# Two-layer cross-attention in float32: layer 0's projections and output sums moved from column halves to row halves of TensorE

## The chip, the cores and the metric

The kernel runs on one core of a Trainium2 chip. The metric is the device time of one execution in microseconds, as the median of several runs. TensorE multiplies matrices, VectorE and ScalarE do the softmax, GpSimd scales rows, and the queue of SyncE (SP) issues nearly all DMA transfers.

## The reference

Four batches of 1024 tokens with 512 features attend to a context of 1024 tokens with 384 features. Two layers follow each other, and all of it is float32:

```python
# layer 0: 16 heads of 64
h = _layernorm(x, gamma, beta)
Q, K, V = h @ Wq, context @ Wk, context @ Wv          # 1024 inner features
attn = softmax(einsum('bihd,bjhd->bhij', Q, K)) * 64 ** -0.5
x = x + einsum('bhij,bjhd->bihd', attn, V) @ Wo + bo
# layer 1: 16 heads of 32, rotated and normalised q and k
xn = x * rsqrt(mean(x * x) + 1e-5) * norm_w
q, k, v = rotate(xn @ wq), rotate(ctx @ wk), ctx @ wv
q, k = q / |q|, k / |k|
x = x + (softmax(q k^T * sqrt(32)) v) @ wout
```

## The kernel before

The work of a batch in layer 0 runs over eight pairs of heads (`p`), and for each pair over eight tiles of 128 queries (`i`): 64 steps a batch. `Attention0.step` (L376) does one step. It first issues the scores of both heads (L367). A head has 64 features, so each of the two score matmuls contracts over 64 rows only, and the two heads run beside each other in the two row halves of the TensorE array. The trace writes this shape 64\*128: 64 rows, 128 columns. The scores take both score tiles, which is all that there is of them (`ps_s`, two buffers of two banks); the next step's scores wait until this step's two exponentials have read them.

Then VectorE takes the negative maximum of each row (L392), ScalarE the exponential and its sum (L393), VectorE the reciprocal (L397), and GpSimd scales the row (L398). In the next step VectorE transposes the result in squares of 32 (L401). After every second step `regroup` (L407) issues 16 DMA copies (L412) that complete the transposition of a block of two query tiles into `eT`. In an odd step, once two blocks wait, `product` (L420) multiplies the older one by the values (L428). That matmul contracts over all 128 rows and fills 64 columns for each head: the column halves, 128\*64 in the trace.

What is left of a step is filled with other work. `Units` (L56) is a queue of small pieces, each with a cost in microseconds. `step` ends with `self.u.fill(us)` (L405): pieces are issued until the budget is used up. The main loop works out the budget as all work still to be done in layer 0, divided by the steps that are left, less the product's 3.5 us in an odd step (L804 to L807), so the fill is spread evenly over the 64 steps. The pieces are:

- keys and queries of a later pair (`pair_units`, L310; `pkT` and `pqT` in the trace), one matmul of 512 columns a piece, three pieces for each half of the keys and four for each half of the queries;
- its values (`pv`), one tile of 128 tokens a piece;
- output sums (`add_units`, L286; `po`): for each of eight token tiles two pieces, and then an addition to the row `x` on VectorE (L295). In pairs 0 and 1 they are those left over from layer 1 of the batch before, and each finished row is stored; from pair 2 on they belong to layer 0, two pairs at a time;
- in pairs 6 and 7 the first rotated keys and values of layer 1 (`rotated_chains`, L452; `value_chains`, L536).

All of these go through the helper `matmul` (L160), which cuts the output features into two column halves in layer 0 (four quarters in layer 1):

```python
        w = P // which["cols"]
        for j in range(which["cols"]):
            rr = slice(j * w, (j + 1) * w)
            nc.tensor.matmul(o[rr], lhsT[:, rr], rhs, start=start, stop=stop)
```

The results of the pieces and of `product` go to four PSUM banks that `bank` (L127) hands out in rotation. `evac` (L136) copies them out on ScalarE.

On SP's queue, in program order, stand the copies of `eT`, the weights of a pair (`pair_load`, L302, three DMAs, two buffers), the rows `x` that are loaded again in pairs 1 and 2 (`load_x`, L279), the output weights (`wo_load`) and the stores of finished rows (`store_all`, after each pair). The weights of pair `p + 1` are asked for where the work on pair `p` begins.

Of the kernel before, what the change touches and what calls it, by code (L numbers as in the profile page):

```python
# [36 lines left out]
P = 128  # L38
S = 1024
# [55 lines left out]

def weave(chains, lag):

    res = []
    for i in range(len(chains) + lag):
        if i < len(chains):  # L100
            res += chains[i][0]
        if 0 < i <= len(chains):
            res += chains[i - 1][1]
        if i >= lag:
            res += chains[i - lag][2]
    return res
# [3 lines left out]
def xattn_kernel(ctx: ExitStack, tc: tile.TileContext, a: dict, out: bass.AP):  # L110
# [14 lines left out]
    which = {"n": 0, "from": 0, "cols": 2, "kept": None}  # L125

    def bank(name):  # L127

        while True:
            which["n"] = which["n"] + 1 if which["n"] < 3 else which["from"]  # L130
            if which["n"] != which["kept"]:
                break
            which["kept"] = None
        return ps_f.tile([P, 512], F32, tag=f"f{which['n']}", name=name)
# [37 lines left out]
    def context_units(b, ct):  # L172

        raws = {}

        def load(h):
            for t in range(4 * h, 4 * h + 4):
                if b == 0 and h:
                    raws[t] = sb.tile([P, S], F32, tag="vals", bufs=4, name=f"c_{b}_{t}")[:, :DC]
                else:  # L180
                    raws[t] = sb.tile([P, DC], F32, tag="row", bufs=4, name=f"c_{b}_{t}")
                nc.sync.dma_start(raws[t], c[b, t * P : (t + 1) * P, :])

        def turn_over(h, k):
            if k == 0:
                if h == 0:
                    both = sb.tile([P, NC_, S], F32, tag="ctxT", bufs=1, name=f"cT_{b}")
                    ct.extend([both[:, :, :512], both[:, :, 512:]])
            pp = bank(f"ptc_{b}_{h}_{k}")
            for t in range(4):  # L190
                nc.tensor.transpose(pp[:, t * P : (t + 1) * P], raws[4 * h + t][:, k * P : (k + 1) * P], ident)
            evac(ct[h][:, k, :], pp)

        return [
            {
                "load": [(0.0, lambda h=h: load(h))],
                "turn": [(0.45, lambda h=h, k=k: turn_over(h, k)) for k in range(NC_)],
            }
            for h in range(2)
        ]  # L200

    def norm_units(b, layer, hT, rows):
# [39 lines left out]
        def turn_over(h, k):  # L242
            if k == 0:
                hT.append(sb.tile([P, NQ, 512], F32, tag="hT", bufs=2, name=f"hT{layer}_{b}_{h}"))
            pp = bank(f"pth{layer}_{b}_{h}_{k}")
            for t in range(4):
                nc.tensor.transpose(pp[:, t * P : (t + 1) * P], got[h][t][:, k * P : (k + 1) * P], ident)  # L247
            if layer == 0:
                nc.scalar.activation(  # L249
                    hT[h][:, k, :], pp, AF.Identity, bias=cols[:, 1, k : k + 1], scale=cols[:, 0, k : k + 1]  # L250
                )
            else:
                nc.scalar.activation(hT[h][:, k, :], pp, AF.Copy, scale=cols[:, 2, k : k + 1])

# [31 lines left out]
    def add_units(xt, lhs, w, name, cs, then=None):  # L286

        n = len(cs)

        def one(t, i, pp=[None]):  # L290
            if i == 0:
                pp[0] = bank(f"{name}_{t}")
            matmul(pp[0], lhs(cs[i])[:, t * P : (t + 1) * P], w(cs[i]), i == 0, i == n - 1)
            if i == n - 1:
                nc.vector.tensor_add(xt[t], xt[t], pp[0])  # L295
                if then is not None:
                    then(t)

        return [[(0.86, lambda t=t, i=i: one(t, i)) for i in range(n)] for t in range(NT)]

# [9 lines left out]
    def pair_units(b, p, w, hT, ct, res):  # L310
# [3 lines left out]
        def project(what, src, w0, nk, h, k, st={}):  # L314
            if what == "kT" and h == 0 and k == 0:
                qk = sb.tile([P, 2, S], F32, tag="qk", bufs=3, name=f"qk0_{n}")
                res["kT"], res["qT"] = qk[:, 0], qk[:, 1]
            if k == 0:
                st["pp"] = bank(f"p{what}0_{n}_{h}")
            matmul(st["pp"], w()[:, w0 + k, :], src[h][:, k, :], k == 0, k == nk - 1)  # L320
            if k < nk - 1:
                return
            if what == "qT":
                evac(res[what][:, h * 512 : (h + 1) * 512], st["pp"])
            else:
                quarters = res[what].rearrange("p (g c i) -> p c g i", g=4, i=32)
                evac(quarters[:, 4 * h : 4 * h + 4], st["pp"].rearrange("p (c g i) -> p c g i", g=4, i=32))

        def values(h, t, st={}):
            if h == 0 and t == 0:  # L330
                res["v"] = sb.tile([P, NT, P], F32, tag="v", bufs=3, name=f"v0_{n}")
            if t == 0:
                st["pp"] = bank(f"pv0_{n}_{h}")
            for k in range(NC_):
                matmul(
                    st["pp"][:, t * P : (t + 1) * P],
                    ct[h][:, k, t * P : (t + 1) * P],
                    w()[:, NQ + NC_ + k, :],
                    k == 0,
                    k == NC_ - 1,  # L340
                )
            if t == 3:
                evac(res["v"][:, 4 * h : 4 * h + 4, :].rearrange("p t f -> p (t f)"), st["pp"])
# [4 lines left out]
            "v": [(0.66, lambda h=h, t=t: values(h, t)) for h in range(2) for t in range(4)],  # L348
# [5 lines left out]
    class Attention0:  # L354


        def __init__(self, b, units):
            self.b, self.u = b, units
            self.blocks = deque()
            self.turn = self.raw = None  # L360
# [15 lines left out]
        def step(self, p, i, pr, us):  # L376
# [28 lines left out]
            self.u.fill(us)  # L405
# [14 lines left out]
        def product(self):  # L420
# [14 lines left out]
            evac(pr["vals"][:, q * W : (q + 1) * W], av[:, :W])  # L435

# [15 lines left out]
    def rotated_chains(dst, src, nk, w, name, tmp):  # L452
# [10 lines left out]
        def project(t0, i, k):  # L463
            if i == 0 and k == 0:
                tiles[t0] = [bank(f"{name}_p{t0}")]
                if which["from"] == 0:
                    which["kept"] = which["n"]
# [7 lines left out]
        def rotate(t0, pp):  # L475
# [16 lines left out]
            tiles[t0] = t1  # L492

        def turn_over(t0):
# [9 lines left out]
            nc.scalar.copy(dst()[:, :, t0 * P : (t0 + TH) * P], pt.rearrange("p (g t) -> p g t", g=2))  # L504

# [30 lines left out]
    def value_chains(v, wv, ct, name):  # L536
        def one(t0, i, k, st={}):
# [5 lines left out]
            if i == TH - 1 and k == NC_ - 1:  # L543
                pv = st["pp"].rearrange("p (t g d) -> p g t d", t=TH, g=2)
                for g in range(2):
                    nc.scalar.copy(v[g][:, t0 : t0 + TH, :], pv[:, g])

# [113 lines left out]
    def prepare_units(b):  # L661

        st = {"ct": [], "hT": [], "pairs": [{} for _ in range(NPAIR)]}
# [5 lines left out]
        def project(p):  # L669
            def begin():  # L670
                if p + 1 < NPAIR:
                    w[p + 1] = pair_load(b, p + 1)

            begin = {"begin": [(0.0, begin)]}
            return begin | pair_units(b, p, lambda: w[p], st["hT"], st["ct"], st["pairs"][p])

        st["project"] = lambda p: flat(project(p).values())
# [50 lines left out]
    for b in range(B):  # L728
        ct, hT, pairs = st["ct"], st["hT"], st["pairs"]
        xt = []  # L730
        att = Attention0(b, work)
# [4 lines left out]
        for p in range(NPAIR):  # L736
# [7 lines left out]
            other = []  # L744
            if p < 2:
                other = tail[p * len(tail) // 2 : (p + 1) * len(tail) // 2]
            elif p % 2 == 0:
                i = p // 2 - 1
                outs = add_units(
# [6 lines left out]
                other = flat(outs[:4])  # L756
            else:
                other = flat(outs[4:])
            if p == 6:
                kq = {}  # L760
# [6 lines left out]
            if p == NPAIR - 1:  # L767
# [14 lines left out]
                other = k[2][0] + k[1][2] + flat(last)  # L782
                values = [(0.0, begin_v)] + vs[0][0] + k[3][0] + reload + k[2][2] + flat(c[0] for c in vs[1:]) + k[3][2]
            ahead = st["project"](p + 2) if p + 2 < NPAIR else []
            n = 7 * (p == 0)
            work.add(ahead[:n] + other)
            if p % 2 or other and p == 0:
                made[p + 1] = work.end()
            work.add(ahead[n:])
            if p + 2 < NPAIR:  # L790
                made[p + 2] = work.end()
            if p == 5:
                wq = []
                work.add([(0.0, lambda wq=wq: wq.append(half_q_load(0)))])
            left = sum(c for c, _ in values) if p == NPAIR - 1 else 0.0
            for i in range(NT):
                if b == 0 and p == 0 and i == 3:
                    work.until(begun)
                if left and i == 4:
                    work.add(values)  # L800
                    left = 0.0
                if 1 <= p <= 2 and i % 2 == 0:
# [3 lines left out]
                todo = work.total() + left + later + AV * ((NT * NPAIR + 1 - max(NT * p + i, 4)) // 2)  # L806
# [4 lines left out]
            if p + 1 < NPAIR:  # L811
                work.until(made[p + 1])
            else:
                work.drain()
            store_all()
# [8 lines left out]
        q = rotated_chains(lambda kq=kq: kq["q"], xnT, NQ, lambda k, wq=wq: wq[0][:, k, :], f"q1_{b}_0", tmp)  # L824
# [7 lines left out]
        which["from"], which["cols"] = 1, 4  # L832
# [63 lines left out]
        which["from"], which["cols"] = 0, 2  # L896
        if b == B - 1:
            tail = flat(adds[1][6:])
        else:
            outs = add_units(  # L900
                xt, lambda n, o=o: o[n], lambda n, w=wo1[1]: w[:, n % 2, :], f"po1_{b}_1", (2, 3), store
            )
            tail = flat(outs)
# [38 lines left out]
```

## Time and profile before

| | us |
|---|---|
| median of 3 runs | 2907.1 (2905.81 to 2908.67) |
| the profiled execution | 2903.31 |
| its span, first to last instruction | 2901.5 |
| TensorE (PE) busy | 2849.7 |
| VectorE (DVE) busy | 2189.1 |
| ScalarE (ACT) busy | 1439.5 |
| GpSimd (POOL) busy | 938.9 |

In the profile PE stands for TensorE's matmuls and PEld for its weight loads. A line of the timeline gives the start and length of a run of like instructions, the engine, the line of the kernel, the operation, what it writes and reads, its shape, and in brackets how long the engine had been idle and what ended that. The ends of matmuls are modelled; their starts are recorded, so the text works with the time from one start to the next. A matmul or weight load in float32 stands in the trace as two instructions.

### The profile page before, as it was taken

How to read it: one execution, taken by the hardware profiler on the slowest of the kernel's cores; microseconds unless marked ns; L12 is line 12 of the kernel's file. 1: busy time of each engine (PE TensorE's matmuls, PEld its weight loads, DVE VectorE, ACT ScalarE, POOL GpSimd, SP SyncE). 2: the span in 40 equal slices, each digit the busy share in tenths (PEclk: the TensorE clock that was granted, in tenths of full speed). 3: DMA queues.
4: the chain of work that ended last, by engine and by line, in shares of the span. 5: the costliest groups of instructions: out<-in, count | busy, mean ns of one | idle time of the engine just before them, and what ended most of it. 6: DMA issues, size and time to landing. Idle time of an engine off the chain costs nothing.

```text
span 2901.5 us, 66687 instructions
## 1 busy us (share of the span) xinstructions
PE 2849.7 (98%) x27336; PEld 1425.7 (49%) x27336; DVE 2189.1 (75%) x2952; ACT 1439.5 (50%) x2329; POOL 938.9 (32%) x776
## 2 busy tenths in 40 slices
PE   8999999999999999999999999999999999999998
PEld 4444455555444444555544445455554444445544
DVE  5677785877777778587777777858877777786877
ACT  4444444666444444466644444446664444444665
POOL 2343353420134335432024433534102343353400
PEclk9999999999999999999999999999999999999999
DMA  5887775010398777401039887730104887773000
GB/s 144 189 187 181 167 171 133 22 37 25 75 210 192 183 170 175 113 22 36 26 92 211 192 184 166 178 93 22 36 26 112 207 197 183 165 171 81 2 2 30
DMA packets 177552, 348.87 MB, mean 120 GB/s; under 512 B 37600, under 2 KB 93152, under 8 KB 177248
## 3 DMA queue, kind: packets, MB, share of 16 engines
q1 hardware_dynamic: 175920, 343.96, 50.1%
q8 instruction: 216, 3.54, 0.5%
q14 instruction: 88, 0.72, 0.1%
q10 hardware_dynamic: 1328, 0.66, 0.1%
HBM read 67.64 MB, written 8.39 MB: 26 GB/s over the span
## 4 chain that ended last, share of the span: by engine, by line
PE 89%; DVE 4%; ACT 3%; issue 2%; SPq 1%; DMA 1%; POOL 1%; DVEq 0%; ACTq 0%
PE s L367 16%; PE av L428 15%; PE po L165 11%; PE s L581 9%; PE pv L165 8%; PE pqT L165 7%; PE av L626 7%; PE pkT L165 5%; PE q_p L165 4%; PE k_p L165 2%; PE av L645 2%; ACT e L591 1%; SPq L412 1%; PE pth L247 1%; DMA eT<-e 1%
## 5 line engine op out<-in xcount | busy, mean ns | idle before, releaser
L392 DVE TENSOR_REDUCE m<-s 128x1 f32<-128x1024 f32 x512 | 602.9, 1219 | 372.1 <-PE s L367 371.5
L591 ACT ACTIVATE e<-s 128x1024 f32<-128x1024 f32 x512 | 496.7, 1022 | 252.5 <-PE s L581 239.5
L398 POOL TENSOR_SCALAR raw<-raw,li 128x1024 f32<-128x1024 f32 x256 | 287.1, 1122 | 725.0 <-DVE li L397 717.0
L367 PE MATMUL s<-qk 64*128 64x512 f32 x2048 | 515.6, 615 | 2.9 <-ACT e L393 2.2
L393 ACT ACTIVATE e<-s,m 128x1024 f32<-128x1024 f32 x256 | 283.1, 1110 | 465.8 <-DVE m L392 224.2
L393 ACT ACTIVATE raw<-s,m 128x1024 f32<-128x1024 f32 x256 | 285.4, 1115 | 455.0 <-DVE m L392 455.0
L428 PE MATMUL av<-eT,v 128*64 128x256 f32 x4096 | 470.1, 382 | 4.8 <-DMA eT<-e 3.6
L398 POOL TENSOR_SCALAR e<-e,li 128x1024 f32<-128x1024 f32 x256 | 287.0, 1122 | 473.7 <-DVE li L397 244.2
L600 DVE TENSOR_TENSOR both<-e 128x512 f32<-128x512 f32 x512 | 340.5, 699 | 87.2 <-ACT e L591 84.3
L428 PEld LDWEIGHTS av<-eT,v 128*64 128x64 f32 x4096 | 284.7, 137 | 225.1 <-issue 84.8
L367 PEld LDWEIGHTS s<-qk 64*128 64x128 f32 x2048 | 183.7, 186 | 281.6 <-issue 165.9
L581 PE MATMUL s<-q,k 32*128 32x256 f32 x4096 | 306.0, 401 | 5.8 <-ACT q L504 2.7
L401 DVE STREAM_TRANSPOSE e<-e 128x1024 f32<-128x1024 f32 x256 | 310.0, 1229 | 0.3
L401 DVE STREAM_TRANSPOSE e<-raw 128x1024 f32<-128x1024 f32 x256 | 310.0, 1228 | 0.2 <-DMA eT<-e 0.2
L581 PEld LDWEIGHTS s<-q,k 32*128 32x128 f32 x4096 | 192.1, 184 | 141.0 <-ACT e L591 72.0
L165 PE MATMUL pqT<-hT,w 128*64 128x512 f32 (+1 forms) x1216 | 240.6, 595 | 2.5 <-ACT hT L249 2.5
L165 PE MATMUL po<-wo,vals 128*64 128x512 f32 x1024 | 234.6, 596 | 0.0
L295 DVE TENSOR_TENSOR x<-x,po 128x512 f32<-128x512 f32 x200 | 131.7, 678 | 86.2 <-PE po L165 85.2
L165 PEld LDWEIGHTS pv<-w,cT 128*64 128x64 f32 (+1 forms) x3360 | 170.3, 132 | 41.6 <-issue 34.8
L165 PE MATMUL pv<-w,cT 128*64 128x128 f32 (+1 forms) x3360 | 184.3, 274 | 0.7 <-ACT hT L249 0.7
L165 PE MATMUL pkT<-cT,w 128*64 128x512 f32 (+1 forms) x912 | 182.4, 598 | 0.0
L602 DVE TENSOR_TENSOR both<-both 128x1024 f32<-128x1024 f32 x128 | 159.7, 1248 | 4.4
(82 smaller groups left out, 2776.1 us busy)
## 6 DMA issues: line engine op xcount, KB each, us to landing
eT<-e SPq DMA_DIRECT2D x2048, 128.0 KB, 2.4
xr<-in_x_dram SPq DMA_DIRECT2D x32, 256.0 KB, 4.0
wo<-in_Wo_dram SPq DMA_DIRECT2D x16, 512.0 KB, 4.5
x<-in_x_dram SPq DMA_DIRECT2D x32, 256.0 KB, 4.0
out_dram<-x SPq DMA_DIRECT2D x32, 256.0 KB, 2.6
w<-in_Wq_dram SPq DMA_DIRECT2D x31, 256.0 KB, 3.2
c<-in_ctx_dram SPq DMA_DIRECT2D x32, 192.0 KB, 4.2
wkv<-in_wkv_dram SPq DMA_DIRECT2D x16, 384.0 KB, 3.5
```

Of the source, the lines that this page charges most:

```text
L165: nc.tensor.matmul(o[rr], lhsT[:, rr], rhs, start=start, stop=stop)
L367: nc.tensor.matmul(sc[j][:, kb * 512 : (kb + 1) * 512], pr["qT"][r[j], i * P : (i + 1) * P], pr["kT"][r[j], kb * 512 : (kb + 1) * 512], st ...
L392: nc.vector.tensor_reduce(m[:, j : j + 1], sc[j], AX.X, ALU.max, negate=True)
L393: nc.scalar.activation(e[j], sc[j].rearrange("p (g s) -> p g s", g=4), AF.Exp, bias=m[:, j : j + 1], accum_out=l[:, j : j + 1])
L398: nc.gpsimd.tensor_scalar(e[j], e[j], li[:, j : j + 1], HD0**-0.5, ALU.mult, ALU.mult)
L401: self.turn = [lambda j=j: nc.vector.transpose(self.e[:, :, i % BQ * 2 + j, :], e[j]) for j in range(2)]
L428: nc.tensor.matmul(av[r[j], :W].rearrange("p (t a i) -> p t a i", t=BQ, a=4), pr["v"][:, k, r[j]], eT[:, j, :, :, k * 32 : (k + 1) * 32], ...
L581: nc.tensor.matmul(sc[j // 2][:, j % 2, c, :], kT[rr, g, k * P : (k + 1) * P], qT[rr, g, qb * WQ : (qb + 1) * WQ], start=True, stop=True,)
L591: nc.scalar.activation(e, sc[u], AF.Exp, scale=float(np.sqrt(np.float32(HD1))))
L600: nc.vector.tensor_add(into[:, 2 * u : 2 * u + 2, :], es[u][:, :, 0, :], es[u][:, :, 1, :])
L602: nc.vector.tensor_add(acc, acc, into)
L626: nc.tensor.matmul(self.av[rr, 0, :], v[g][:, 2 * kk + c, rr], es[j // 2][:, j % 2, c, :], start=first and c == 0, stop=end and c == 1,)
```

## The change

The keys and queries of pairs 2 to 7 and the output sums of pairs 0 to 5 are issued in another form and at other places.

- A *duo* makes two outputs at once, each in its own bank: both token halves of a pair's keys or queries, or two token tiles of the output sums. The contraction over 128 rows is cut into two row halves. In the duo's first half one output takes rows 0 to 63 and the other rows 64 to 127, in the array's two row halves; in the second half they change places. The number of matmuls stays the same.
- A duo's first half is issued in the gap of one even step and its second half in the gap of the next even step, before the first half of the duo that follows. The two banks stay taken over the odd step between. At the end both outputs are copied on ScalarE, or added to `x` on VectorE.
- Even steps then hold duo halves, odd steps the product and one piece of the old queue (two if over four are waiting). The duos begin at step 2 of a batch, in batch 0 at step 10; before that and after the last duo the old rule fills the steps. The value pieces of pair `p + 2` join the queue at step 3 of pair `p`.
- The values of a pair come in pieces of two token tiles, each with a bank and a copy of its own.
- `bank` hands out the bank that was released longest ago; `let_go` releases one when the instruction that empties it has been issued.
- The weights of a pair are asked for when the work of the pair before in the same buffer has been issued (`then`, run at the next fill). Layer 1's first half of `wq` is asked for after pair 6's work. Stores are issued at the start of even steps.
- In pairs 6 and 7 the pieces stand in another order, and the first values of layer 1 join the queue at step 3 of pair 7 in place of 4.

```diff
+class Duos:
+    SLOT = 0.86
...
+    def half(self, i):
+        n, f = self.open
+        f(i)
+        if i:
+            self.open = None
+        return n * self.SLOT
+
+    def fill(self):
+        us = self.half(1) if self.open else 0.0
+        if self.todo:
+            self.open = self.todo.popleft()
+            us += self.half(0)
+        return us
...
     def bank(name):
-        while True:
-            which["n"] = which["n"] + 1 if which["n"] < 3 else which["from"]
-            if which["n"] != which["kept"]:
-                break
+        if free[0] == which["kept"] and len(free) > 1:
+            free.rotate(-1)
             which["kept"] = None
+        which["n"] = free.popleft()
...
+    def let_go(pp):
+        free.append(taken.pop(id(pp))[0])
...
+    def duo(names, n, lhsT, rhs, close):
+        pps = []
+        def half(i):
+            if i == 0:
+                pps.extend(bank(name) for name in names)
+            for k in range(n):
+                for t in range(2):
+                    o = t ^ i
+                    rr = slice(t * 64, (t + 1) * 64)
+                    nc.tensor.matmul(
+                        pps[o], lhsT(o, k)[rr], rhs(o, k)[rr], start=i == 0 and k == 0, stop=i == 1 and k == n - 1
+                    )
+            if i == 1:
+                for o in range(2):
+                    close(o, pps[o])
+                    let_go(pps[o])
+        return n, half
...
-            "v": [(0.66, lambda h=h, t=t: values(h, t)) for h in range(2) for t in range(4)],
+            "v": [(1.32, lambda h=h, t=t: values(h, t)) for h in range(2) for t in (0, 2)],
+            "duos": [project_duo("kT", ct, NQ, NC_), project_duo("qT", hT, 0, NQ)],
...
-            self.u.fill(us)
+            self.fill(i % BQ, us)
...
+            def then():
+                if 1 <= p < NPAIR - 2:
+                    st["due"].append(lambda: w.update({p + 2: pair_load(b, p + 2)}))
+                elif p == NPAIR - 2:
+                    st["due"].append(lambda: st["wq"].append(half_q_load(0)))
...
+        def fill(odd, us, b=b, duos=duos, st=st):
+            while st["due"]:
+                st["due"].popleft()()
+            if not duos.begun:
+                work.fill(us)
+            elif odd:
+                for _ in range(min(1 + (len(work.todo) > 4), len(work.todo))):
+                    work.one()
+            else:
+                alone = not duos.open
+                work.owed = us - duos.fill()
+                if alone or not duos.open:
+                    work.fill(0.0)
...
-                other = k[2][0] + k[1][2] + flat(last)
-                values = [(0.0, begin_v)] + vs[0][0] + k[3][0] + reload + k[2][2] + flat(c[0] for c in vs[1:]) + k[3][2]
+                other = k[2][0] + k[1][2] + flat(last[:2]) + k[3][0] + flat(last[2:]) + k[2][2]
+                values = [(0.0, begin_v)] + vs[0][0] + reload + vs[1][0] + k[3][2] + vs[2][0] + vs[3][0]
...
+                ahead = st["project"](p + 2)
+                duos.add(ahead["duos"][:1] + sums[:1] + ahead["duos"][1:] + sums[1:])
...
+                if i == 3 and p < NPAIR - 2:
+                    work.add(ahead["v"])
+                    made[p + 2] = work.end()
+                    left = 0.0
...
+                if i % 2 == 0:
+                    store_all()
...
+                duos.begun = duos.total() > 0 and NT * p + i >= (2 if b else NT + 2)
```

## The prediction

> **What bounds the kernel now.** I read the page first: engines, granted clock, chain.
>
> ```profile
> PE 2849.7 (98%) x27336; PEld 1425.7 (49%) x27336; DVE 2189.1 (75%) x2952; ACT 1439.5 (50%) x2329; POOL 938.9 (32%) x776
> PEclk9999999999999999999999999999999999999999
> PE 89%; DVE 4%; ACT 3%; issue 2%; SPq 1%; DMA 1%; POOL 1%; DVEq 0%; ACTq 0%
> ```
>
> TensorE (PE) is the bound, at full clock. A busy PE is not a PE at its peak, so next the timeline of one even and one odd step of layer 0 (columns: start, length).
>
> ```profile
> 299.33 1.99 PE L367 MATMUL s<-qk 64*128 64x512 f32 x8
> 299.87 0.19 PEld L367 LDWEIGHTS s<-qk 64*128 64x128 f32 x2 [0.24 <-issue]
> 300.30 0.19 PEld L367 LDWEIGHTS s<-qk 64*128 64x128 f32 x2 [0.23 <-issue]
> 301.25 4.51 PE L165 MATMUL pqT<-hT,w 128*64 128x512 f32 x20
> 302.16 0.14 PEld L165 LDWEIGHTS pqT<-hT,w 128*64 128x64 f32 x2 [0.28 <-issue]
> 302.59 0.14 PEld L165 LDWEIGHTS pqT<-hT,w 128*64 128x64 f32 x2 [0.28 <-issue]
> ...
> 305.69 1.99 PE L367 MATMUL s<-qk 64*128 64x512 f32 x8
> ...
> 307.61 3.67 PE L428 MATMUL av<-eT,v 128*64 128x256 f32 x32
> ...
> 311.11 1.48 PE L165 MATMUL pv<-w,cT 128*64 128x128 f32 x24
> ...
> 312.52 1.99 PE L367 MATMUL s<-qk 64*128 64x512 f32 x8
> ```
>
> The trace has every f32 matmul twice; matmuls run in pairs, and the weight loads tick at 0.43 us a pair in both shapes, 64\*128 (row halves) and 128\*64 (column halves). Scores are 4 pairs, 1.72 us, but take 1.92 from start to start; pqT is 10 pairs, 4.30, and takes 4.44 (299.33, 301.25, 305.69). So going into row halves and back costs 0.20 + 0.14, about 0.35 us. In the odd step: 0.20, av 3.50 against 16 pairs of 0.2165 (3.46), pv 1.41 against 12 of 0.109 (1.31): again 0.34. From av to pv, both in column halves, nothing is lost. Each of the 64 steps of a batch pays one such round trip: 22 us a batch.
>
> The next view asks how short a step can be when PE has little to do:
>
> ```profile
> 1144.29 2.21 PE L367 MATMUL s<-qk 64*128 64x512 f32 x8
> ...
> 1145.47 1.26 DVE L295 TENSOR_TENSOR x<-x,po 128x512 f32<-128x512 f32 x2
> 1146.43 3.67 PE L428 MATMUL av<-eT,v 128*64 128x256 f32 x32
> 1146.65 2.35 DVE L392 TENSOR_REDUCE m<-s 128x1 f32<-128x1024 f32 x2
> ...
> 1149.05 1.10 ACT L393 ACTIVATE e<-s,m 128x1024 f32<-128x1024 f32 x1
> 1150.03 2.25 PE L367 MATMUL s<-qk 64*128 64x512 f32 x8
> ```
>
> With av alone the step takes 5.74: the score tiles come free only after the second exponential. The reduces began 2.36 after the scores instead of 2.02 (299.33 to 301.35 in the step above), held by the x sums; without that the step is 5.40. I use 5.45; the ends are 5.40 and 5.74. Last, batch 1's opening and PE's wait list:
>
> ```profile
> 755.65 4.81 PE L165 MATMUL pv<-w,cT 128*64 128x128 f32 x84
> ...
> 763.01 4.46 PE L165 MATMUL pkT<-cT,w 128*64 128x512 f32 x20
> ```
> ```profile
> PE av L428 <- DMA eT<-e: 3.6, 2, 2.5
> ```
>
> Today the opening gaps are full, because fill is spread evenly over all 64 steps.
>
> **The change, part by part.** Numbers of steps are within a batch, 0 to 63.
>
> *Switches removed.* With duos begun, an even step has scores and duo halves, all in row halves; only odd steps switch. Duos run from step 2 in batches 1 to 3 and from step 10 in batch 0, one opened per even step: 24 duos a batch (6 of keys, 6 of queries, 12 of sums), 20 in batch 0. The last is opened at step 48 and closed at 50, where column units follow. So even steps 2 to 48 lose their trip (24), and step 1 has no fill at all (25); batch 0 loses 20. That is 95 × 0.35 = 33.2 us off the path.
>
> *What a duo half costs.* Matmuls are as many as before. I take 0.43 a pair, from the scores rows. Here a rule speaks against the change: the Trainium skill, TensorE: Matmul & The Clock Gate, section Part 3: Packing small matmuls, says that a weight load overlaps matmuls in flight only when its row group differs. Each duo pair reloads both row groups, as do the scores, at 0.186 a load. By the rule each pair would cost up to 0.186 more; there are 12 pairs in a key duo, 16 in a query duo, 8 in a sum duo: 264 a batch, 232 in batch 0, 1024 in all: 190 us more. By the trace it is nothing: the scores pairs above reload the same halves and still tick at 0.43. I take 0.
>
> *Gaps that run dry.* Now I count what is left to fill. Even gaps hold two halves: 1.72 + 2.58 or 1.72 + 3.44; even steps are 6.02 or 6.88. An odd step is 1.72 + 3.46 + one value unit (12 pairs, 1.31) + 0.35 = 6.84. Both exceed 5.45. But in batches 1 to 3 step 0 takes all four waiting value units, so step 1 has scores alone (1.72), step 2 a first half alone (4.30), step 3 one value unit and no av yet (3.38): short of 5.45 by 3.73 + 1.15 + 2.07. Pair 6's step 54 has three units (4.65): 0.80. That is 7.75 a batch. In batch 0 it is steps 8 (one value unit, 2.07), 10 (a first half, 1.15) and 54 (0.80): 4.0. Total 3 × 7.75 + 4.0 = 27.3 us given back. With 5.74 it is 32, with 5.40 it is 26.5.
>
> A second rule bears on step 1, where PE rests 3.5 us. The same page, Part 1, says that an idle window of some 3.4 us halves the clock until a busy one has passed. PE's waits of 2.45 us (35.37 to 37.82) and 2.50 us (before the av at 105.44) left the clock at 0.999. By the rule, up to 1.7 us in each of three batches, 5 in all; by the trace 0. I take 0 and keep 5 for the range.
>
> *Banks.* The half that opens takes the banks of the odd step's av and value unit; their copies end long before. The av takes the first bank of the duo just closed: by keys or queries it is copied 6.33 after the even step's scores began (ACT is free at 5.75, a copy is 0.58), by sums it is added at 7.4 (DVE's own chain ends at 6.76, two adds 1.26); av starts at 6.02 + 1.92 = 7.94 or later. So 0. If that cover of 0.5 is gone, PE stands at av with the value unit and the next scores behind it, once per pair.
>
> *DVE.* Two x sums come together and hold DVE until 8.02; the next reduce can start at 8.04. A delay is covered by the odd step's 6.84 against 5.45. Cost 0.
>
> *Value units* are split: two ACT copies near 0.38 instead of one of 0.58, ACT 50% busy: 0. *SP.* Pair loads now go when the previous pair of that buffer is finished, stores at even steps, the half Wq load a pair later. The order on SP stays: 16 copies of eT (10.0 us from 6.78 after the scores, 2.4 to land, so 19.2) with weights (1.7), x (0.6) and stores (0.6) between them; av needs them three steps later plus 1.92: 20.8 to 22.5 in the steady part, 18.8 at step 5 and 18.4 at batch 0's step 11. That gives new waits of 0.4 to 1 at the first and 1 to 3 at the second. Before, such waits were 2.50 in batch 0 and 1.11 in batch 2 (the list's 3.6), and 1.1 put down to issue: 4.7. I set old against new: 0, with ±4.
>
> *Last two pairs.* The steps around the rotated keys are stretched now by waits for the turned tiles and the rotation on DVE: in batch 1, 6.33 for av alone (1117.02 to 1123.35) and 8.20 for the step after. Summed against pairs × pitch, about 2.3 a batch, 1.2 in batch 0: 8 us. The new order puts a turn 2 to 4 steps behind its projection and starts the last values at step 59. I take half of it: −4; bounds 0 and −8.
>
> **Sum.** −33.2 + 27.3 + 0 − 4 = −9.9 us. The profiled execution was 2903.3 (span 2901.5, 1.8 around it), 3.8 below the median 2907.1. Against the median: 2897.
>
> **The rivals.** *A wash (0.21).* Starved steps cost 5.74 and the tail's waits stay: −33.2 + 32 = −1: 2906, own range 2901 to 2913. For it: the starved step shown took 5.74, and the one beside a rotation 6.33. Against it: steps 1 to 3 have no x sums or rotation.
>
> *The duo halves are slower than the scores (0.24).* The one mechanism that ends slower: a duo pair accumulates into a bank that the other row half used, with fresh weights, and no row of the trace does that. Place: every even gap. Price: 1024 pairs. It decides at 10 ns a pair (of 430), which eats the gain; at 16 ns it is slower by 0.2%, at 22 ns 2910 + 9 = 2919. For it: the rule above. Against it: column pairs accumulate at 0.43 and row pairs reload at 0.43.
>
> *More than the sum (0.10).* All 8 us of the tail's waits and the 5 of eT go too: −33.2 + 27.3 − 13 = −19: 2888.
>
> *The change does not do what it says*: if column work slipped into even gaps the switches would stay. The fill rule sends column units to an even step only when no duo is open, so I give this nothing of its own.
>
> **How the numbers follow.** My forecast 0.45: 2897, own range 2889 to 2901. Measurement can tell about 0.2%, 5.8 us. Faster by more: forecast and the third rival, less 0.02 for the forecast's upper edge: 0.53. Within: the wash, 0.22. Slower: 0.25. Range for 8 in 10: 2882 to 2919, down past the third rival, up to the slower one's 22 ns.
>
> **What would show it.** Right: in even steps of pairs 1 to 5 the duo's matmuls appear as 64\*128 right after the scores, scores take 1.72 to the next start, and even steps are 6.0 and 6.9; odd ones 6.8. Scores to scores in steps 1 to 3 near 5.45. Wrong: weight loads of duos ticking above 0.43; PE waiting at av for ACT or DVE; a granted clock below full after step 1; steps 1 to 3 above 5.8.

## The result, and the profile after

| | us |
|---|---|
| kernel before, median of 12 runs | 2909.9 |
| changed kernel, median of 12 runs | 2911.3 (2905.8 to 2916.0) |
| ratio | 1.0007, 95% interval 0.9998 to 1.0016 |
| profiled execution after | 2905.83 |
| its span | 2904.0 |

No difference that can be measured, where 10 us of gain were forecast. The page after:

```profile
PE 2831.5 (98%) x27336; PEld 1505.8 (52%) x27336; DVE 2186.0 (75%) x2952; ACT 1447.7 (50%) x2393; POOL 936.5 (32%) x776
PEclk9999999999999999999999999999999999999999
PE 85%; SPq 4%; DVE 4%; ACT 2%; issue 2%; DMA 2%; POOL 1%; ACTq 0%; DVEq 0%
```

PE is busy 18 us less and the span is 2.5 us longer, so PE waits more. The chain says for whom: SP's queue (SPq) and DMA rise from 1% each to 4% and 2%. An even and an odd step of the steady part, in the timeline:

```profile
287.17 1.99 PE L485 MATMUL s<-qk 64*128 64x512 f32 x8
288.99 1.88 PE L356 MATMUL po<-wo,vals 64*128 64x512 f32 x8
288.99 0.19 PEld L356 LDWEIGHTS po<-wo,vals 64*128 64x128 f32 x2 [0.23 <-issue]
289.42 0.19 PEld L356 LDWEIGHTS po<-wo,vals 64*128 64x128 f32 x2 [0.24 <-issue]
...
290.71 3.60 PE L356 MATMUL pqT<-hT,w 64*128 64x512 f32 x16
...
294.14 1.88 PE L485 MATMUL s<-qk 64*128 64x512 f32 x8
...
295.95 3.67 PE L546 MATMUL av<-eT,v 128*64 128x256 f32 x32
...
299.46 1.48 PE L206 MATMUL pv<-w,cT 128*64 128x128 f32 x24
...
300.87 1.99 PE L485 MATMUL s<-qk 64*128 64x512 f32 x8
```

Weight loads tick at 0.43 in the duo too. The even step lasts 6.97 (287.17 to 294.14) for 16 pairs, 6.88; the odd one 6.73. In the kernel before the two were 6.36 for 14 pairs, 6.02, and 6.83: together they have lost one round trip, as was meant. What remained in the forecast were the starved steps, in which PE has too little to do, and the waits. Batch 1's step 1, scores alone:

```profile
759.73 1.99 PE L485 MATMUL s<-qk 64*128 64x512 f32 x8
...
763.06 1.11 ACT L511 ACTIVATE e<-s,m 128x1024 f32<-128x1024 f32 x1 [2.85 <-DVE m L510]
...
764.17 1.10 ACT L511 ACTIVATE e<-s,m 128x1024 f32<-128x1024 f32 x1
...
764.32 2.65 PE L485 MATMUL s<-qk 64*128 64x512 f32 x7 [2.61 <-ACT e L511]
```

It lasts 4.59: the next scores begin when the first exponential has freed one tile, and do not wait for the second. But the second tile comes later, and the step that follows pays for it, as after batch 0's step 8:

```profile
81.69 1.99 PE L485 MATMUL s<-qk 64*128 64x512 f32 x8
83.61 1.53 PE L206 MATMUL pv<-w,cT 128*64 128x128 f32 x24
86.29 3.11 PE L485 MATMUL s<-qk 64*128 64x512 f32 x8 [1.15 <-ACT raw L511]
```

Step 8 lasts 4.60, and in step 9 PE stands 1.15 us among the scores. The rows of PE's wait list for av, before (its other row, 3.6, stands in the prediction) and after, and SP's (total, times, longest):

```profile
PE av L428 <- issue: 1.1, 1, 1.1
```
```profile
PE av L546 <- DMA eT<-e: 8.8, 7, 2.7
PE av L546 <- DVE m L510: 6.8, 3, 3.0
PE av L546 <- DMA x<-in_x_dram: 0.7, 1, 0.7
PE av L546 <- DVE x L370: 0.5, 1, 0.5
PE av L546 <- issue: 0.2, 1, 0.2
```
```profile
SPq L324 <- DMA out_dram<-x: 22.3, 12, 2.7
```

Together 4.7 before and 17.0 after. The second row of after names VectorE, which had long been done; it is the same wait for eT, as the place shows: all these waits fall on step 11 of batch 0 and on steps 5, 11, 15 and 23 of batches 1 to 3. SP's line is new: 12 times a reload of `x` held the queue until the store out of the same buffer had landed. Batch 1's step 20, first SP, then PE:

```profile
877.82 11.14 SPq L530 DMA_DIRECT2D eT<-e  x16
889.07 0.52 SPq L391 DMA_DIRECT2D w<-in_Wk_dram  x1
...
890.98 0.99 SPq L990 DMA_DIRECT2D out_dram<-x  x2
894.72 0.34 SPq L324 DMA_DIRECT2D x<-in_x_dram  x1
895.16 10.04 SPq L530 DMA_DIRECT2D eT<-e  x16
```
```profile
903.70 1.88 PE L485 MATMUL s<-qk 64*128 64x512 f32 x8
908.03 3.67 PE L546 MATMUL av<-eT,v 128*64 128x256 f32 x32 [2.45 <-DVE m L510]
```

The copies of step 20 (its scores began at 883.89) could have started 6.78 later, at 890.67. They started at 895.16, behind weights, two stores and a reload that stood at the head of the queue from 891.97 to 894.72. Three steps on, the av stands 2.45 us. In the same trace three waits of PE were followed by 3.41 us at half clock: two such waits for eT (2.71 in batch 0, 3.02 in batch 3) and the 2.61 after batch 2's step 1. Three windows around step 23 of batch 3 (a plain step, the wait, what follows), and one after batch 2's step 1; the third number from the end is PE's granted clock:

```profile
2327.06:2333.79 6.73, 6.73 (x67) 4.16 (x63) 5.38 (x8) 3.19 (x7) 2.92 (x3) 1.00 0.75 236
2340.76:2345.66 4.90, 1.88 (x11) 0.61 (x7) 3.37 (x5) 0.03 (x1) 0.99 (x1) 1.00 0.89 209
2345.66:2352.26 6.60, 6.60 (x57) 5.04 (x57) 2.55 (x4) 2.65 (x5) 2.23 (x2) 0.74 0.89 217
1482.00:1488.00 6.00, 5.46 (x16) 2.39 (x18) 4.78 (x7) 2.50 (x5) 2.23 (x2) 0.72 0.00 0
```

Av and values take 6.60 here where 4.92 is usual (295.95 to 300.87). The balance, profile against profile, in us:

| | forecast | read from the two traces |
|---|---|---|
| switches | −33.2 | −33.2 |
| starved steps | +27.3 | +22 |
| waits for eT | 0 | +12.3 |
| half clock | 0 | +4.6 |
| last two pairs | −4 | −3.0 |
| sum | −9.9 | +2.7; the span grew by 2.5 |

The third column comes about as follows. *Excess* is here the time of a step beyond its pairs × pitch. Switches: 95 trips of 0.35; in steps 26 to 49 the excess fell by 4.2 a batch, over 12 even steps. Starved steps: the excess of steps 1 to 5 of batches 1 to 3 and of steps 8 to 11 of batch 0, less trips, waits for eT and half clock; about 6.2 in each of the three batches and 3.8 in batch 0. Half clock: 1.7, 1.2 and 1.7 at the three places; the half clock in the last microseconds of both executions is left out. Last two pairs: the excess of steps 50 to 62, 28.6 before and 25.6 after.

### The profile page after: what moved, and what is told of

The parts are those of the page before. It is cut to its first block, busy times and chain, and to the rows that moved or that the text cites. A ratio compares the mean times of both kernels' runs of the same rounds, so it can differ in the third digit from the quotient of the medians.

```text
span 2904.0 us, 66765 instructions
## 1 busy us (share of the span) xinstructions
PE 2831.5 (98%) x27336; PEld 1505.8 (52%) x27336; DVE 2186.0 (75%) x2952; ACT 1447.7 (50%) x2393; POOL 936.5 (32%) x776
## 4 chain that ended last, share of the span: by engine, by line
PE 85%; SPq 4%; DVE 4%; ACT 2%; issue 2%; DMA 2%; POOL 1%; ACTq 0%; DVEq 0%
PE s L485 15%; PE av L546 15%; PE s L703 9%; PE pv L206 8%; PE av L748 7%; PE po L206 6%; PE pqT L356 5%; PE po L356 4%; SPq L530 4%; PE q_p L206 4%; PE pkT L356 3%; PE k_p L206 2%; PE av L767 2%; PE pqT L206 2%; PE pkT L206 1%
## 5 line engine op out<-in xcount | busy, mean ns | idle before, releaser
L485 PE MATMUL s<-qk 64*128 64x512 f32 x2048 | 522.4, 608 | 11.0 <-ACT e L511 9.0
L546 PEld LDWEIGHTS av<-eT,v 128*64 128x64 f32 x4096 | 290.7, 137 | 235.2 <-issue 81.1
L485 PEld LDWEIGHTS s<-qk 64*128 64x128 f32 x2048 | 194.7, 186 | 240.2 <-issue 179.0
L356 PE MATMUL pqT<-hT,w 64*128 64x512 f32 x768 | 172.8, 589 | 0.0
L760 DVE RECIPROCAL rest<-rest 128x256 f32<-128x256 f32 x64 | 111.9, 1749 | 43.0 <-ACT rest L768 43.0
L356 PE MATMUL pkT<-cT,w 64*128 64x512 f32 x576 | 137.2, 590 | 0.0
L748 PE MATMUL av<-e,v 128*32 128x256 f32 x2048 | 137.0, 385 | 0.0
```

Source lines behind the costliest of these rows:

```text
L356: nc.tensor.matmul(pps[o], lhsT(o, k)[rr], rhs(o, k)[rr], start=i == 0 and k == 0, stop=i == 1 and k == n - 1)
L485: nc.tensor.matmul(sc[j][:, kb * 512 : (kb + 1) * 512], pr["qT"][r[j], i * P : (i + 1) * P], pr["kT"][r[j], kb * 512 : (kb + 1) * 512], st ...
L546: nc.tensor.matmul(av[r[j], :W].rearrange("p (t a i) -> p t a i", t=BQ, a=4), pr["v"][:, k, r[j]], eT[:, j, :, :, k * 32 : (k + 1) * 32], ...
L748: nc.tensor.matmul(self.av[rr, 0, :], v[g][:, 2 * kk + c, rr], es[j // 2][:, j % 2, c, :], start=first and c == 0, stop=end and c == 1,)
```

## The experiments

Three theories stood against each other. *Theory 1*: the row form saves what was forecast, and it is given back at starved steps and in waits that SP's order makes. *Rival 1*: the row form is worth nothing. *Rival 2*: eT is late because the DMA engines are loaded, whatever the order. *Rival 3*: idle steps are made up for later. Times below are medians of 4 to 16 runs, ratios are to the kernel before in the same session.

### Duo halves in columns, nothing else changed (e1_columns)

```diff
             for k in range(n):
-                for t in range(2):
-                    o = t ^ i
-                    rr = slice(t * 64, (t + 1) * 64)
-                    nc.tensor.matmul(
-                        pps[o], lhsT(o, k)[rr], rhs(o, k)[rr], start=i == 0 and k == 0, stop=i == 1 and k == n - 1
-                    )
+                matmul(pps[i], lhsT(i, k), rhs(i, k), k == 0, k == n - 1)
```

> The changed kernel with every duo half made in column halves: the first half makes the first output whole (all 128 rows, two column halves), the second half the second. Number of matmuls, places in the gaps, banks, queue and loads are unchanged. Theory 1 (the row form saves the switch between row and column halves, 0.35 us in each of 95 even steps; what it saved was lost again at starved steps and in waits of av for eT): 20 to 33 us slower than the changed kernel, 2930 to 2945, the lower end because longer even steps give eT more time. Rival 1 (the row form is worth nothing, all differences come from where the work is placed): within 5 us of 2911.

Measured: 2934.7, ratio 1.0092 (1.0079 to 1.0106); 23 us slower than the changed kernel. A step of its timeline:

```profile
305.41 1.99 PE L480 MATMUL s<-qk 64*128 64x512 f32 x8
307.33 3.65 PE L206 MATMUL pqT<-hT,w 128*64 128x512 f32 x16
310.81 1.89 PE L206 MATMUL po<-wo,vals 128*64 128x512 f32 x8
312.63 1.99 PE L480 MATMUL s<-qk 64*128 64x512 f32 x8
```

The same 16 pairs last 7.22 (305.41 to 312.63) against 6.97, and the odd steps are 0.1 longer too (6.83): the round trip is back. Rival 1 falls. Not all of 33 us shows, because longer even steps give eT time: PE's av rows sum to 8.3 in this trace, not to 17.0, and 33.2 less these 8.7 is 24.5. So the row form itself, by shortening the steps, makes about 9 us of waits.

### The reload of x behind the copies (e2_x_behind)

```diff
-                if 1 <= p <= 2 and i % 2 == 0:
-                    load_x(b, xt, 4 * (p - 1) + i // 2)
...
                 att.step(p, i, pairs[p], max(todo / n - now, 0.0))
+                if 1 <= p <= 2 and i % 2 == 0:
+                    load_x(b, xt, 4 * (p - 1) + i // 2)
```

> The changed kernel with the reload of x in pairs 1 and 2 issued behind the step's eT copies in place of ahead of them. Theory 1: in the changed kernel the copies of the even steps 12 and 20 start 9.8 to 11.3 us after the scores and not 6.8, because the reload of x stands ahead of them on SP and waits for the store of the same row; av then waits 0.7 to 3.0 us at steps 15 and 23. With the reload behind, the copies start at 6.8, these waits go: 8 to 12 us faster than the changed kernel, 2899 to 2903. Rival 2 (the copies land late because the DMA engines are loaded in pairs 1 and 2, whatever the order on SP): within 4 us of 2911, waits where they were.

Measured: 2897.0, ratio 0.9959 (0.9947 to 0.9971), 14 us below the changed kernel and more than forecast. Two lines moved, and the kernel is faster than the one before. SP's waits for `out_dram` at the reload are gone from the list, and the queue around the same step 20 reads:

```profile
886.62 0.42 SPq L990 DMA_DIRECT2D out_dram<-x  x1
887.39 0.35 SPq L324 DMA_DIRECT2D x<-in_x_dram  x1
887.85 0.40 SPq L990 DMA_DIRECT2D out_dram<-x  x1
888.36 11.39 SPq L530 DMA_DIRECT2D eT<-e  x16
```

The copies start 8.4 after their scores, not 11.3, and av waits 1.7 at step 23. At step 11 the waits of batches 1 to 3 went too. PE's av rows sum to 8.6, 8.4 less; the mean granted clock of the runs has a median of 0.998, where the changed kernel's has 0.996. By an estimate 0.002 of 2900 us is some 6 us, and with the 8.4 that makes the 14. Not all waits went (1.5 us in batch 2's step 15): weights and stores still stand ahead of a block. Rival 2 falls for the larger part; for the waits that stayed it was not tested (the DMA share in the windows above is 0.89, in the plain step 0.75).

### Duos from step 0 (e3_from_0), and both edits (e4_both)

```diff
-                duos.begun = duos.total() > 0 and NT * p + i >= (2 if b else NT + 2)
+                duos.begun = duos.total() > 0 and NT * p + i >= (0 if b else NT + 2)
```

> The changed kernel with the duos of batches 1 to 3 beginning at step 0 in place of step 2. Theory 1: PE's idle time in steps 1 to 3 falls from about 4.9 us a batch to about 1.5, the wait of the first av (1.1) goes, but the queue runs dry two steps earlier at steps 53 to 55, about 1.5 a batch; rows of layer 1 are stored two steps earlier, so some of the waits at steps 15 and 23 go too: 6 to 14 us faster than the changed kernel, 2897 to 2905. Rival 3 (idle steps are made up for later anyway, the end is set by the tail of the batch): within 4 us of 2911.

Measured: 2896.7, ratio 0.9958 (0.9944 to 0.9972), 15 us below the changed kernel. Two things change at once here: the opening of a batch is fuller, and the stores come two steps sooner. The waits at step 23 are gone without touching the reload; batches 2 and 3 have none at steps 5 to 23, and PE's av rows sum to 4.8, 12 less. The fuller opening gains some 10 us in steps 1 to 5, waits for eT and half clock apart, but the excess of steps 50 to 62 grows by 9, over three batches. So rival 3 falls by its number, but its reason holds in large part: the idle steps moved to the end of the batch, and what was gained are the waits.

> Both edits: the reload of x behind the copies, and the duos from step 0 in batches 1 to 3. Theory 1: 12 to 20 us faster than the changed kernel, 2891 to 2899, and faster than the kernel before. Rival 2 and 3: no more than 4 us faster than the changed kernel.

Measured: 2893.9, ratio 0.9944 (0.9932 to 0.9957). 17 us below the changed kernel, as forecast, but only 3 below either edit alone, within what these runs can tell: both edits heal largely the same wait. Its trace shows what the earlier start costs at the other end. The queue of pieces runs dry at steps 53 to 55, here in batch 1:

```profile
1107.41 2.14 PE L485 MATMUL s<-qk 64*128 64x512 f32 x8
1109.48 1.08 PE L206 MATMUL po<-wo,vals 128*64 128x512 f32 x4
1112.01 4.72 PE L485 MATMUL s<-qk 64*128 64x512 f32 x8 [1.45 <-ACT raw L511]
1116.66 5.40 PE L546 MATMUL av<-eT,v 128*64 128x256 f32 x32
```

Scores of 1.99 take 4.72 and an av of 3.67 takes 5.40. The windows of the same place give the clock:

```profile
1112.00:1120.00 8.00, 7.98 (x24) 3.24 (x26) 7.21 (x10) 3.50 (x6) 2.96 (x3) 0.59 0.70 156
```

Of its six runs the three with a mean clock of 0.995 or 0.996 took 2896.4 to 2896.9, the three with 0.998 took 2888.3 to 2891.5.

### Pair 6 given more to do (e5_tail), and batch 0 from step 8 (e6_tail_8)

```diff
+                other += k[2][0] + k[1][2]
...
-                other = k[2][0] + k[1][2] + flat(last[:2]) + k[3][0] + flat(last[2:]) + k[2][2]
+                other = flat(last[:2]) + k[3][0] + flat(last[2:]) + k[2][2]
```

This is added to both edits; the first line stands in pair 6, the others in pair 7.

> The kernel with both edits (x behind the copies, duos from step 0 in batches 1 to 3), and in addition the rotated keys of chain 2 and the turn of chain 1 handed to the queue in pair 6 in place of pair 7. Theory 1 (PE rests in steps 53 to 55 because the queue is empty there, and the clock is halved after it): the dry steps 53 and 54 are filled, the two stretches of half clock of 6.8 us at steps 53 to 55 of batches 1 and 2 go; 6 to 14 us faster than with both edits alone, 2880 to 2888, mean clock 0.998 or more. Rival (the tail is bound by the rotation on the vector engine, not by an empty queue): within 3 us of 2894.

Measured: 2887.1, ratio 0.9916 (0.9903 to 0.9930), 7 us below both edits alone. The clock of its runs is 0.999 to 1.0, where the changed kernel's are 0.995 to 0.998. This version beats both kernels: 0.84% under the kernel before. In the traces most of the gain is clock: the two stretches of 6.83 us at half clock are gone, while the excess of steps 50 to 62 is 9.1 in a batch, where batch 3 of e4_both, which has no half clock there, had 9.6. So the rival falls by its number, but what bounds the tail itself stays open.

`e6_tail_8` is `e5_tail` with `NT` in place of `NT + 2` in the line that sets `duos.begun`.

> As the kernel before in this call, and in addition the duos of batch 0 beginning at step 8 in place of 10. Theory 1: in batch 0 steps 8 to 10 last 6.0, 5.5 and 7.7 us in place of 4.6, 6.6 and 4.6 and carry work that came later, and the av of step 11 waits under 1 us for eT in place of 3.5 to 4: 2 to 6 us faster than the kernel before in this call. Rival (the wait at step 11 is the start-up of the copies, whatever the steps last): within 1 us of it.

Measured: 2888.0, ratio 0.9921 (0.9908 to 0.9935): no gain over e5_tail. Yet the wait went. The changed kernel at batch 0's step 11, then this one:

```profile
97.53 3.11 PE L485 MATMUL s<-qk 64*128 64x512 f32 x8
103.35 5.36 PE L546 MATMUL av<-eT,v 128*64 128x256 f32 x32 [2.71 <-DMA eT<-e]
```
```profile
101.99 2.04 PE L485 MATMUL s<-qk 64*128 64x512 f32 x8
103.95 3.67 PE L546 MATMUL av<-eT,v 128*64 128x256 f32 x32
```

Its profiled span is 3.0 us shorter (2883.3 against 2886.3), but the medians do not show it. My forecast missed; the rival's reason, a start-up of the copies, is not what the trace shows either. Why the medians agree stays open.

### The best version with its duo halves in columns (e8_columns_tail)

> The kernel with x behind the copies, duos from step 0 and the fuller pair 6 (run as e5_tail), with its duo halves made in column halves as in e1_columns. Theory 1: there the row form had its full price hidden in part by waits for eT; where few waits are left, columns cost nearly the full 0.35 us in each of some 92 to 95 even steps: 28 to 33 us slower than e5_tail, 2915 to 2920, no better than the kernel before. Rival 1 (the gain of e5_tail over the kernel before comes from the new placement, not from the row form): within 12 us of 2887.

Measured: 2920.9, ratio 1.0031 (1.0022 to 1.0040). The two ratios, 1.0031 and 0.9916, differ by 0.0115 of some 2912 us: 33 us. With the waits alike in both (PE's av rows sum to 7.6 and 7.9) the row form gives the whole 95 × 0.35 = 33.2. The placement by itself, its three corrections included, makes the kernel 9 us slower than before (0.0031 × 2912), so the gain is the form's, not the placement's.

## Why the prediction was wrong, point by point

*Switches removed*: right. 95 trips of 0.35; the steps after have the predicted lengths within 0.1 (6.11 and 6.97 for 6.02 and 6.88; 6.73 for 6.84), and the last experiment measures 33 us. *What a duo half costs*: right at 0.43; the rule that a reload in the same row group doesn't overlap did not hold here, and the rival that rested on it would have cost over 10 ns a pair.

*SP* is the step that failed. I set the old waits for eT against the new at 0 ± 4. They grew from 4.7 to 17.0 us, +12.3; steps 11 and 23 of batches 1 to 3, which had none before, have 10 of it. With the clock below it is more than the whole gain that was forecast. The prediction's own figures left no room: the copies need 19.2 us after the scores, 22.1 with weights, x and stores between them, and av comes at 20.8 to 22.5. And I had each DMA's length and the order, but not what stands at the head: that the reload of a row waits for the store out of the same buffer to land, that the duos close the last rows of layer 1 at steps 14 and 18 where the old pieces were done at step 10, and that 16 copies stand behind. Moving the reload took 8.4 us of the waits away.

*Gaps that run dry*: mechanism right, places right (steps 1 to 3, 8 and 10), size nearly: for these places the prediction has 24 us and the traces 22. Its other 3 us were for step 54, which was not starved: it held four pieces, not three. But 5.45 came out well by luck. In the step that I read it from, scores and av filled PE for 2.14 + 3.60 = 5.74: PE was the bound. The trace after gives 4.59, and the rest is paid one step later, where the scores wait for the second exponential (1.15 at step 9).

*The clock* is the second term that I put at nothing: I took 0 and kept 5 for the range. It cost 4.6 in the profile. The rule that I set aside (the Trainium skill, TensorE: Matmul & The Clock Gate, Part 1) had given up to 5, but for step 1 of three batches and after an idle window of some 3.4 us. Only one of the three halvings follows a step 1; two follow waits for eT; and the waits were 2.61 to 3.02 long. So its number was near by luck. The median run lost more than the profiled one: that one, at 0.998, was the shortest of the 12, and the median clock was 0.996.

*Last two pairs*: −4 was taken for less waiting, and −3.0 came. *Banks, DVE, value units*: 0 in the steady steps, as predicted.

Of the rivals, the wash has 2911 in its own range of 2901 to 2913, but by luck: it let starved steps cost 32, and they cost 22, and it let the tail's waits stay, and they shrank.

## What to carry to other kernels

Where two shapes of TensorE tiling alternate, look at start-to-start times against pairs × pitch: a constant excess a step is the price of the switch, and putting all of one shape into one gap removes it. Such a regrouping moves everything else: trace for each DMA that is moved what it waits for and what stands behind it in its queue. Where copies have little room before their reader, shorter steps turn into waits. And before a step's length is taken as the floor of a chain, check that no engine fills it, and count the step that follows too.

## What the runs showed that I had not expected

The clock was halved after idle times well under 3.4 us: after waits of 2.61, 2.71 and 3.02 in the changed kernel, and in e4_both after one of 1.45 in a stretch of thin steps, there for 6.83 us. The same wait does not always do it: batch 1's step 1 waited 2.61 as well, and the clock stayed. The time of a run followed it: the three runs of the changed kernel with a mean clock of 0.995 took 2913.6 to 2916.0, the two with 0.998 took 2905.8 and 2910.7. And the two row halves run apart. In batch 1's step 2, behind seven of the eight scores (the line at 764.32 above), stand:

```profile
766.39 0.59 PE L356 MATMUL pkT<-cT,w 64*128 64x512 f32 x1
766.81 0.59 PE L485 MATMUL s<-qk 64*128 64x512 f32 x1
```

So one half begins the next gap's work while the other still runs the scores. The first score tile comes free 1.11 us before the second there (exponentials at 763.06 and 764.17).
